# A two-layer graph network on one core: the second attention transposed through DRAM, and three smaller changes

## The chip, the cores and the metric

The kernel runs on one core of a Trainium2 chip. TensorE (PE in the profile; PEld is its weight load) multiplies matrices into PSUM; VectorE (DVE), ScalarE (ACT) and GpSimd (POOL) work element by element; SyncE (SP) issues DMAs. Each engine executes its own list of instructions in order, and waits on semaphores for the others. The metric is the device time of one execution in microseconds. Three runs of the kernel before took 2780.21, 2780.91 and 2783.22 us, median 2780.91.

## The reference

`x` has 64 batches of 256 tokens with 512 features, in float32; `adj` is a 256 x 256 matrix of zeros and ones. Two layers are applied, each with a residual and a layer norm without weights.

```python
# layer 0: eight heads of 64, masked by adj
q, k, v = x @ Wq + bq, x @ Wk + bk, x @ Wv + bv          # per batch 256 x 512
scores = q_h @ k_h.T / 8 + (1 - adj) * -1e9
x = layernorm(x + softmax(scores) @ v @ Wo + bo)
# layer 1: additive graph attention
h = x @ W
e = leaky_relu(s1[:, None] + s2[None, :], 0.2) * adj     # s1 = h @ a1, s2 = h @ a2
x = layernorm(x + elu(softmax(e) @ h + beta * h))
```

## The kernel before

**Tiling.** A batch is two token tiles of 128 partitions (`NT` = 2). Two batches make a pair; q, k and v are computed for a pair (`pair`, L570), everything after them for one batch (`batch`, L634), s = 0 or 1 within the pair. All operands are float32. A product of a weight and the tokens is done in seven block products in place of eight (`project`, L414): sums of weight quarters are kept or streamed from DRAM, and sums of token quarters are made by GpSimd (`token_sums`, L393).

**First layer of a batch.** `scores(c)` (L699) gives transposed scores of two heads; VectorE adds the mask, ScalarE takes the exponential (`pT`), GpSimd adds the two key halves (`both`). `denominators` (L723) sums over keys by TensorE, so that row 16h of the result holds the sums of head h; VectorE takes the reciprocal of the 128 x 256 tile (L735), SyncE stores eight of its rows to DRAM (L746) and loads them back spread over the partitions of their heads (L750). `mix` multiplies by v, `onto` scales by the reciprocals (L776), and the product with Wo is added to `X`, which holds x plus biases.

**Norm.** `norm` (L553) takes one token tile: `bn_stats` and `bn_aggr` on VectorE, two GpSimd operations for the reciprocal root, one of VectorE for the offset, and ScalarE's normalising pass. It is called for each tile after the first layer (L867) and by `finish` (L646) after the second.

**Second layer of a batch.** Since h = xW, s1 and s2 are x times two fixed rows, `wa_sb`; four VectorE products with accumulation give them per token in `sv` (L877). s2 is needed as a row on all partitions: TensorE transposes the broadcast columns (`tr_s`, L887). Then `z` = s1 + s2, leaky ReLU, the mask by GpSimd, maximum, exponential, reciprocal and a scaled sum with beta on the diagonal (L896 to L918) give `e`, the attention of 256 x 256. TensorE transposes it in four blocks (`tr_a`, L923), ScalarE copies it to `attT` (L927), GpSimd makes its quarter sums (L963), and `spread` multiplies it with x, `u` with W. `finish` applies the ELU, adds and norms.

**The first tokens.** x is needed transposed. `blocks` (L583) loads x with the 32 x 32 blocks in transposed places, in runs of 32 elements, four issues for one batch, and one VectorE instruction transposes within the blocks (L591).

**The order.** Nothing is launched as written: each operation is recorded by `plan.op(engine, ns, fn, reads, writes, ...)` with a planned duration, and `Plan.place` (L112) simulates the engines and buffers, and from that fixes the order of every engine's list. TensorE's order is prescribed: `turn(what)` gives each operation a round (the pair's number plus `LATER[what]`) and the place of `what` in `ROUND`; the last 60 TensorE operations are free. The other engines take what can start earliest, ties by a due time derived from TensorE's order. A transfer is planned to land 2200 ns after its issue (`LAG`). Buffers come from pools with fixed numbers of places (`slots`): 18 of the kind `half`, four of `full`, eight PSUM banks. `claims` makes an operation take places for buffers that later ones write.

```python
ROUND = ("sums1", "mix1", "scores0", "v", "o1", "attention0", "u1", "x", "spread0", "sums0", "mix0", "scores1", "q",
         "logits1", "o0", "u0", "attention1", "k", "spread1", "logits0")
```

With `LATER`, a round holds steps of several pairs: sums1, o1, logits1 of the pair before, u1 of the one before that, q and k of the next. So the latency of one batch's steps lies beside TensorE's work for the others. The last batch (`last`) has shorter paths of its own.

## Time and profile before

| what | value |
|---|---|
| runs | 2780.21, 2780.91, 2783.22 us |
| profiled execution | 2782.27 us, span 2780.4 us |
| TensorE clock granted | 0.995 of full speed |
| second layer's transposes on TensorE | 256 `tr_a`, 128 `tr_s` matmuls |
| reciprocal L735 on VectorE | 64, 1757 ns each |
| norm statistics on VectorE | 256 of 681 ns, 256 of 169 ns |
| norm's two GpSimd operations | 256 of 245 ns, 256 of 607 ns |
| VectorE's block transpose of x, L591 | 64, 1232 ns each |
| DMA engines' mean busy share, main queue | 34.0%, 256.96 MB |

How to read it: a span is the time from the first to the last instruction of the profiled execution; the execution's own time is a little longer. A group of instructions stands on one line: line of the kernel, engine, operation, output and inputs by name, shape, count, then the busy time in microseconds and the mean of one in nanoseconds, then the idle time before it with what ended it. A timeline line has the start and the duration in microseconds, then the same names. A line on waits has who waited, for whom, the total in microseconds, how many times, and the longest.

### The profile page before, as it was taken

The page shows a single profiled execution, that of the slowest core. Times are in us where ns is not written, and L with a number is a line of the kernel's source. Part 1 is how long each engine was busy: PE and PEld are TensorE (multiplying, and loading weights), DVE is VectorE, ACT ScalarE, POOL GpSimd, SP SyncE. Part 2 cuts the span into 40 slices and gives each one's busy share as a digit, 9 for nine tenths or more (in the row PEclk, how much of TensorE's full clock was granted, in tenths as well). Part 3 has the DMA queues.
Part 4 walks back from the last instruction along what each step waited for, and adds up shares of the span by engine and source line. Part 5 has one row for each costly group of instructions (what it writes and reads, how often), then busy time and mean ns, then how long its engine had stood idle before and what let it go on. Part 6 is the DMA issues. An engine that isn't in the chain of part 4 may idle for free.

```text
span 2780.4 us, 46736 instructions
## 1 busy us (share of the span) xinstructions
PE 2738.3 (98%) x16259; PEld 2312.2 (83%) x16259; DVE 2067.6 (74%) x4190; ACT 1238.7 (45%) x2747; POOL 1759.1 (63%) x2379
## 2 busy tenths in 40 slices
PE   7999999999999999999999999999999999999997
PEld 6788888888888888888888888888888888888875
DVE  6777777787776777777877767777778777677777
ACT  2344444454454444444544544444445445444443
POOL 5666666666666666666666666666666666666664
PEclk9999999999999999999999999999999999999998
DMA  8333332343332433323433324433234332243211
GB/s 220 88 96 107 81 103 68 101 115 96 84 85 80 115 107 80 103 69 100 114 96 84 84 80 114 107 81 102 68 101 115 95 85 85 81 114 92 62 50 36
DMA packets 429313, 260.02 MB, mean 94 GB/s; under 512 B 279448, under 2 KB 360592, under 8 KB 429072
## 3 DMA queue, kind: packets, MB, share of 16 engines
q1 hardware_dynamic: 428944, 256.96, 34.0%
q8 instruction: 132, 2.16, 0.3%
q14 instruction: 109, 0.89, 0.1%
q0 software_dynamic: 128, 0.01, 0.0%
HBM read 220.73 MB, written 36.17 MB: 92 GB/s over the span
## 4 chain that ended last, share of the span: by engine, by line
PE 97%; DVE 2%; issue 0%; SPq 0%; POOL 0%; DMA 0%; ACT 0%; POOLq 0%; DVEq 0%; ACTq 0%
PE ps_chain L433 33%; PE ps_cross L433 22%; PE ps_pair L433 10%; PE ps_sc L708 8%; PE ps_pv L685 8%; PE ps_second L433 6%; PE ps_fourth L433 6%; PE ps_den L731 2%; PE tr_a L923 1%; PE tr_s L887 0%; DVE junk L877 0%; SPq L588 0%; PE ps_y L938 0%; DVE x L650 0%; PE ps_plain L497 0%
## 5 line engine op out<-in xcount | busy, mean ns | idle before, releaser
L719 POOL TENSOR_TENSOR both<-pT 128x256 f32<-128x256 f32 x512 | 369.2, 749 | 46.2 <-ACT pT L717 46.2
L717 ACT ACTIVATE pT<-pT 128x512 f32<-128x512 f32 x512 | 296.5, 625 | 113.6 <-DVE pT L715 113.4
L715 DVE TENSOR_TENSOR pT<-ps_sc,maskT_sb 128x512 f32<-128x512 f32 x512 | 318.1, 679 | 0.2 <-PE ps_sc L708 0.2
L560 POOL TENSOR_SCALAR rs<-mv 128x1 f32<-128x1 f32 x256 | 62.7, 245 | 351.7 <-DVE mv L557 342.8
L708 PE MATMUL ps_sc<-qT,kT 64*128 64x256 f32 x2048 | 238.4, 382 | 0.0
L685 PE MATMUL ps_pv<-pT,v 128*64 128x256 f32 x2048 | 235.1, 382 | 0.0
L708 PEld LDWEIGHTS ps_sc<-qT,kT 64*128 64x128 f32 x2048 | 192.8, 187 | 44.4 <-issue 24.2
L685 PEld LDWEIGHTS ps_pv<-pT,v 128*64 128x64 f32 x2048 | 141.3, 137 | 91.0 <-issue 25.9
L566 ACT ACTIVATE x<-x,nmr,rs 128x512 f32<-128x512 f32 x256 | 204.0, 811 | 8.1 <-DVE nmr L564 6.5
L877 DVE SCALAR_TENSOR_TENSOR junk<-x,wa_sb 128x512 f32<-128x512 f32 x256 | 195.4, 800 | 0.0
L404 POOL TENSOR_TENSOR yS<-yT 128x256 f32<-128x256 f32 x126 | 103.4, 820 | 144.1 <-DVE yT L478 139.1
L910 ACT ACTIVATE e<-e,nm 128x256 f32<-128x256 f32 x128 | 64.7, 506 | 255.5 <-DVE nm L907 255.5
L561 POOL TENSOR_TENSOR rs<-rs,neg_half 128x1 f32<-128x1 f32 x256 | 155.3, 607 | 21.3
L669 POOL TENSOR_TENSOR x<-x,res_sb 128x512 f32<-128x512 f32 x128 | 161.7, 1284 | 7.8 <-DMA x<-in_x_dram 6.4
L556 DVE BATCH_NORM_STATS2 bn<-x 128x6 f32<-128x512 f32 x256 | 164.2, 681 | 2.2
L963 POOL TENSOR_TENSOR X_sums<-x 128x256 f32<-128x256 f32 x126 | 107.1, 850 | 66.4 <-ACT x L566 66.4
L927 ACT COPY attT<-tr_a 128x512 f32<-128x512 f32 x64 | 37.5, 586 | 244.3 <-PE tr_a L923 243.9
L404 POOL TENSOR_TENSOR xS<-xT 128x512 f32<-128x512 f32 x64 | 81.7, 1277 | 92.6 <-PE ps_chain L433 83.0
L404 POOL TENSOR_TENSOR oS<-oT 128x256 f32<-128x256 f32 x126 | 98.1, 779 | 65.9 <-DVE oT L776 59.7
L905 POOL TENSOR_TENSOR e<-e,adj_sb 128x512 f32<-128x512 f32 (+1 forms) x65 | 82.1, 1263 | 85.5 <-DVE e L902 84.1
L771 ACT COPY oT<-ps_pv 128x512 f32<-128x512 f32 x128 | 75.1, 586 | 131.8 <-PE ps_pv L685 129.6
L433 PE MATMUL ps_chain<-sw_sb,yS 128*128 128x256 f32 x504 | 129.3, 379 | 0.0
(230 smaller groups left out, 7260.1 us busy)
## 6 DMA issues: line engine op xcount, KB each, us to landing
xin<-in_x_dram SPq DMA_DIRECT2D x256, 128.0 KB
x<-in_x_dram SPq DMA_DIRECT2D x64, 512.0 KB
out_dram<-x SPq DMA_DIRECT2D x128, 256.0 KB
inv_all<-rows SPq DMA_DIRECT2D x126, 256.0 KB
wq_sums<-wq_sums SPq DMA_DIRECT2D x124, 256.0 KB
wk_sums<-wk_sums SPq DMA_DIRECT2D x124, 256.0 KB
wq_sums<-in_L_gnn_Wq_dram SPq DMA_DIRECT2D x93, 256.0 KB
wk_sums<-in_L_gnn_Wk_dram SPq DMA_DIRECT2D x93, 256.0 KB
```

Of the source, the lines that this page charges most:

```text
L404: plan.op("POOL", 180 + 545 * width // P, lambda: nc.gpsimd.tensor_tensor(dst(), p(), m(), ALU.subtract), reads, writes)
L433: nc.tensor.matmul(dst[:, f, :], lhs, rhs, start=start and f == 0 and c == 0, stop=c == inner - 1, skip_group_check=True)
L556: plan.op("DVE", 690, lambda: nc.vector.bn_stats(bn[A], X[:, t, :]), [(X, (t, 0)), (X, (t, 1))], [bn])
L561: nc.gpsimd.tensor_tensor(rs[A], rs[A], neg_half, ALU.pow)
L566: plan.op("ACT", 810, lambda: nc.scalar.activation(X[:, t, :], X[:, t, :], AF.Identity, bias=nm[A], scale=rs[A]), [nm, rs], [(X, (t, 0)), ...
L669: plan.op("POOL", 1270, lambda t=t: nc.gpsimd.tensor_tensor(X[:, t, :], X[:, t, :], res_sb[A], ALU.add), [res_sb], tokens(t))
L685: nc.tensor.matmul(acc[r * HD:(r + 1) * HD, i, :], V[:, 2 * k + s, h * HD:(h + 1) * HD], pT[h][:, k, :], start=k == 0, stop=k == NT - 1)
L708: nc.tensor.matmul(acc[j][:, k, :], kT[r:r + HD, c, key_blk(k)], own(qT, r, c), start=True, stop=True)
L715: plan.op("DVE", 690, lambda h=h, i=i: nc.vector.tensor_add(pT[h][A], acc[i][A], maskT_sb[A]), [acc[i], maskT_sb], [pT[h]])
L717: plan.op("ACT", 620, lambda h=h: nc.scalar.activation(pT[h][A], pT[h][A], AF.Exp, scale=1.0 / HD ** 0.5), [pT[h]], [pT[h]])
L719: plan.op("POOL", 725, lambda h=h, i=i: nc.gpsimd.tensor_tensor(both[c][:, i, :], pT[h][:, 0, :], pT[h][:, 1, :], ALU.add), [pT[h]], [(bot ...
L877: plan.op("DVE", 780, lambda t=t, i=i, junk=junk: nc.vector.scalar_tensor_tensor(junk[A], X[:, t, :], 1.0, wa_sb[:, i, :], op0=ALU.mult, o ...
```

## The change

Five things are altered.

1. For all but the last batch the attention `e` is stored to DRAM (`square`) and loaded in four strided issues with its 32 x 32 blocks in transposed places (`att_b`); one VectorE instruction transposes within the blocks into `attT`. TensorE's four transposes and ScalarE's copy go. The step keeps a place in TensorE's order, with no instruction in it.
2. The row of logits s2 is stored to DRAM from `sv` (`line`, 256 single elements) and loaded as a row on all partitions (`row`), in place of two TensorE transposes.
3. `norm` takes both token tiles at once: sums by ScalarE's accumulator, then squares of the difference from the mean likewise, one small scaling by VectorE, three GpSimd operations on 128 x 2, and ScalarE's normalising passes. `finish` does both tiles before it norms; the last batch still goes tile by tile.
4. The denominators are copied by ScalarE as they are, stored to DRAM, loaded as 128 x 16 (`few`), inverted there, stored again and then spread.
5. The first pair's x is loaded plainly and transposed by TensorE (`turned`). `ROUND` has another order, new pools `few`, `line` and `square` are declared, and some planned durations differ.

```diff
-ROUND = ("sums1", "mix1", "scores0", "v", "o1", "attention0", "u1", "x", "spread0", "sums0", "mix0", "scores1", "q",
-         "logits1", "o0", "u0", "attention1", "k", "spread1", "logits0")
+ROUND = ("sums1", "mix1", "scores0", "u1", "attention0", "v", "spread0", "o1", "sums0", "mix0", "scores1", "u0", "x",
+         "logits1", "attention1", "q", "o0", "logits0", "k", "spread1")
...
-    def norm(X, t):
-        bn, mv, rs, nm = st(6, "bn"), st(2, "mv"), st(1, "rs"), st(1, "nmr")
-        plan.op("DVE", 690, lambda: nc.vector.bn_stats(bn[A], X[:, t, :]), [(X, (t, 0)), (X, (t, 1))], [bn])
-        plan.op("DVE", 175, lambda: nc.vector.bn_aggr(mv[A], bn[A]), [bn], [mv])
+    def norm(X, ts):
+        n = len(ts)
+        sums, mean, sq, rs, nm = (st(n, name) for name in ("sum", "mean", "sq", "rs", "nmr"))
+        def total(i, t, func, to, bias):
+            junk = sb("half", [D], "junk")
+            plan.op("ACT", 700, lambda: nc.scalar.activation(
+                junk[A], X[:, t, :], func, bias=mean[:, i:i + 1] if bias else 0.0, accum_out=to[:, i:i + 1]),
+                [(X, (t, 0)), (X, (t, 1))] + ([mean] if bias else []), [junk, (to, i)])
+        for i, t in enumerate(ts):
+            total(i, t, AF.Identity, sums, False)
+        plan.op("DVE", 110, lambda: nc.vector.tensor_scalar(mean[A], sums[A], -1.0 / D, None, ALU.mult), [sums], [mean])
+        for i, t in enumerate(ts):
+            total(i, t, AF.Square, sq, True)
         def rsqrt():
-            nc.gpsimd.tensor_scalar(rs[A], mv[:, 1:2], EPS, None, ALU.add)
-            nc.gpsimd.tensor_tensor(rs[A], rs[A], neg_half, ALU.pow)
-        plan.op("POOL", 800, rsqrt, [mv], [rs])
-        plan.op("DVE", 150, lambda: nc.vector.scalar_tensor_tensor(
-            nm[A], mv[:, 0:1], -1.0, rs[A], op0=ALU.mult, op1=ALU.mult), [mv, rs], [nm], mode="two")
-        plan.op("ACT", 810, lambda: nc.scalar.activation(
-            X[:, t, :], X[:, t, :], AF.Identity, bias=nm[A], scale=rs[A]),
-            [nm, rs], [(X, (t, 0)), (X, (t, 1))])
+            nc.gpsimd.tensor_scalar(rs[A], sq[A], 1.0 / D, EPS, ALU.mult, ALU.add)
+            nc.gpsimd.tensor_tensor(rs[A], rs[A], neg_half[A].to_broadcast([P, n]), ALU.pow)
+            nc.gpsimd.tensor_tensor(nm[A], mean[A], rs[A], ALU.mult)
+        plan.op("POOL", 1000, rsqrt, [sq, mean], [rs, nm])
+        for i, t in enumerate(ts):
+            plan.op("ACT", 810, lambda i=i, t=t: nc.scalar.activation(
+                X[:, t, :], X[:, t, :], AF.Identity, bias=nm[:, i:i + 1], scale=rs[:, i:i + 1]),
+                [nm, rs], [(X, (t, 0)), (X, (t, 1))])
...
+        def turned(s):
+            rows = sb("xin", [NT, D], f"xin_{m}_{s}")
+            for t in range(NT):
+                plan.op("SP", 700, lambda t=t: nc.sync.dma_start(rows[:, t, :], dram(x, s)[:, t, :]), [], [(rows, t)],
+                        first=s == 0 and t == 0)
+                tr = ps([C, P], "tr_x")
+                def pe(t=t, tr=tr):
+                    for c in range(C):
+                        nc.tensor.transpose(tr[:, c, :], rows[:, t, blk(c)], ident)
+                plan.op("PE", 430, pe, [(rows, t)], [tr], claims=[xT])
+                plan.op("ACT", 680, lambda t=t, tr=tr: nc.scalar.copy(xT[:, :, blk(2 * t + s)], tr[A]), [tr],
+                        [(xT, (t, s))])
...
         turn("x")
-        plan.op("PE", 0, lambda: None, [], [(xT, "turn")], claims=[xT])
-        for s in range(2):
-            blocks(s)
+        if m == 0:
+            for s in range(2):
+                turned(s)
+        else:
+            plan.op("PE", 0, lambda: None, [], [(xT, "turn")], claims=[xT])
+            for s in range(2):
+                blocks(s)
...
-        def finish(t, us, u, mode):
...
-            norm(X, t)
-            plan.op("SP", 1400, lambda: nc.sync.dma_start(
-                dram(out, s)[:, t, :], X[:, t, :]), tokens(t), [])
+        def finish(ts, us, u, mode):
+            for t in ts:
...
+            norm(X, ts)
+            for t in ts:
+                plan.op("SP", 700, lambda t=t: nc.sync.dma_start(dram(out, s)[:, t, :], X[:, t, :]), tokens(t), [])
...
-            rows = Buf(dram_pool, "rows", [H, N], "rows")
+            rows = Buf(dram_pool, "rows", [2, H, N], "rows")
...
-                plan.op("DVE", 1750, lambda: nc.vector.reciprocal(inv[A], acc[A]), [acc], [inv])
...
+                def sum_of(i, src, n, to):
+                    plan.op("ACT", 240 + n, lambda: nc.scalar.activation(
+                        to[:, 0:n], src[:, 0:n], AF.Identity, accum_out=range_sb[:, i, b:b + 1]), [src],
+                        [to, (range_sb, (i, b))])
-                plan.op("SP", 60, lambda: nc.sync.dma_start(rows[A], inv[0:P:P // H, :]), [inv], [rows])
+                n = H * N // P
+                few, one = sb("few", [n], "few"), sb("few", [n], "one")
+                sum_of(0, acc, N, inv)
+                plan.op("SP", 500, lambda: nc.sync.dma_start(rows[0], inv[0:P:P // H, :]), [inv], [(rows, 0)])
+                plan.op("SP", 500, lambda: nc.sync.dma_start(
+                    few[A], rows[0].rearrange("h (a n) -> (h a) n", n=n)), [(rows, 0)], [few])
+                plan.op("DVE", 190, lambda: nc.vector.reciprocal(few[A], few[A]), [few], [few])
+                sum_of(1, few, n, one)
+                plan.op("SP", 500, lambda: nc.sync.dma_start(
+                    rows[1].rearrange("h (a n) -> (h a) n", n=n), few[A]), [few], [(rows, 1)])
...
-                    plan.op("SP", 1500, spread, [rows], [(everywhere, i)])
+                    plan.op("SP", 1000, spread, [(rows, 1)], [(everywhere, i)])
...
-        for t in range(NT):
-            norm(X, t)
+        for ts in ([0], [1]) if last else ([0, 1],):
+            norm(X, ts)
...
-        sv = [st(2, "s") for t in range(NT)]
+        sv = st(2 * NT, "s")
...
-                    accum_out=sv[t][:, i:i + 1]), tokens(t) + [(wa_sb, i)], [junk, (sv[t], i)],
+                    accum_out=sv[:, NT * i + t:NT * i + t + 1]), tokens(t) + [(wa_sb, i)], [junk, (sv, (i, t))],
...
-        row = ps([N], "tr_s")
-        def pe_row():
-            for t in range(NT):
-                nc.tensor.transpose(row[:, blk(t)], sv[t][:, 1:2].to_broadcast([P, P]), ident)
...
+        attT = sb("half", [NT, N], "attT")
+        s2 = [(sv, (1, t)) for t in range(NT)]
         turn("logits")
-        plan.op("PE", 220, pe_row, sv, [row], claims=[z, e])
+        if last:
+            row = ps([N], "tr_s")
+            def pe_row():
+                for t in range(NT):
+                    nc.tensor.transpose(row[:, blk(t)], sv[:, NT + t:NT + t + 1].to_broadcast([P, P]), ident)
+            plan.op("PE", 220, pe_row, s2, [row], claims=[z, e])
+        else:
+            line, row = Buf(dram_pool, "line", [N], "line"), sb("half", [N], "row")
+            plan.op("PE", 0, lambda: None, [], [(row, "turn")], claims=[z, e, row])
+            with_turn = [(row, "turn")]
+            plan.op("SP", 500, lambda: nc.sync.dma_start(
+                line[A].rearrange("(t p) -> p t", p=P), sv[:, NT:2 * NT]), s2 + with_turn, [line])
+            plan.op("SP", 500, lambda: nc.sync.dma_start(row[A], row_on_all(line[A], 0, N)), [line], [row])
...
-                z[:, t, :], row[A], sv[t][:, 0:1], None, ALU.add), [row, sv[t]], [(z, t)])
+                z[:, t, :], row[A], sv[:, t:t + 1], None, ALU.add), [row, (sv, (0, t))], [(z, t)])
...
-            def pe_att(ts=ts):
-                for j in range(NT):
-                    for t in range(NT)[ts]:
+        turn("attention")
+        if last:
...
+        else:
+            square, att_b = Buf(dram_pool, "square", [N, N], "square"), sb("half", [NT, N], "att_b")
+            plan.op("PE", 0, lambda: None, [], [(att_b, "turn")], claims=[attT, att_b])
+            plan.op("SP", 500, lambda: nc.sync.dma_start(
+                square[A].rearrange("(t p) j -> p t j", p=P), e[A]), [e], [square])
+            for f in range(4):
+                plan.op("SP", 720, lambda f=f: nc.sync.dma_start(
+                    att_b[f * 32:(f + 1) * 32].rearrange("p k (b i) -> p k b i", i=32),
+                    square[A].rearrange("(b j) (k f i) -> f j k b i", j=32, f=4, i=32)[f]),
+                    [square, (att_b, "turn")], [(att_b, f)])
+            plan.op("DVE", 660, lambda: nc.vector.transpose(attT[A], att_b[A]), [att_b], [(attT, i) for i in range(4)])
...
-        for t in range(NT):
-            finish(t, [(u, (t, 0)), (u, (t, 1))], lambda t=t: u[:, t, :], "two")
+        finish(range(NT), lambda t: [(u, (t, 0)), (u, (t, 1))], lambda t: u[:, t, :], "two")
```

## The prediction

> **What bounds the kernel now.** I read the page's head and chain first, then who TensorE waited for, then its timeline in the steady middle, then the DMA queue there, and last the two ends.
>
> ```profile
> span 2780.4 us, 46736 instructions
> PE 2738.3 (98%) x16259; PEld 2312.2 (83%) x16259; DVE 2067.6 (74%) x4190; ACT 1238.7 (45%) x2747; POOL 1759.1 (63%) x2379
> ...
> PE 97%; DVE 2%; issue 0%; SPq 0%; POOL 0%; DMA 0%; ACT 0%; POOLq 0%; DVEq 0%; ACTq 0%
> ```
>
> A busy share alone proves little, but the chain that ended last is 97% TensorE as well. The waits of TensorE give the rest: each occurs once, so none belongs to the loop.
>
> ```profile
> PE ps_chain L433 <- DVE xT L591: 12.5, 1, 12.5
> PE ps_chain L433 <- DVE pT L715: 6.4, 1, 6.4
> PE ps_pair L433 <- DVE nmr L564: 4.0, 1, 4.0
> PE tr_a L923 <- POOL rs L560: 3.6, 1, 3.6
> ```
>
> The first is the start, the second the filling of the pipeline (65 to 71.5 us), the last two lie after 2700 us. In between, TensorE's instruction list sets the time. The chain in order of time shows the same head's scores 84.95 us apart in successive pairs of batches; 31 to 32 such rounds make the span.
>
> ```profile
> 1246.94 3.65 PE ps_sc L708 x32
> 1295.68 3.65 PE ps_sc L708 x32
> 1331.89 3.65 PE ps_sc L708 x32
> ```
>
> TensorE's timeline shows what the second layer's transposes take: the distance from their start to the next group's start (printed durations overlap, since matmuls are pipelined).
>
> ```profile
> 1231.68 1.03 PE L433 MATMUL ps_chain<-so_sb,oS 128*128 128x256 f32 x4
> 1232.54 0.60 PE L923 MATMUL tr_a<-ident,e 128*128 128x128 f32 x4
> 1232.98 1.03 PE L433 MATMUL ps_chain<-w_sb,yT 128*128 128x256 f32 x4
> ...
> 1262.71 0.38 PE L887 MATMUL tr_s<-ident,s 128*128 128x128 f32 x2
> 1262.93 1.03 PE L433 MATMUL ps_chain<-wo_sb,oT 128*128 128x256 f32 x4
> ```
>
> So four transposes of the attention take 0.44 us and the two of the row of logits 0.22 us.
>
> The DMA queue, for the price of a hop through DRAM:
>
> ```profile
> 1242.24 2.80 SPq L588 DMA_DIRECT2D xin<-in_x_dram  x4
> 1245.70 0.62 SPq L746 DMA_DIRECT2D rows<-inv  x1
> 1247.59 1.30 SPq L750 DMA_DIRECT2D inv_all<-rows  x2
> ```
>
> A store to DRAM followed by a load of it costs 1247.59 - 1245.70 = 1.9 us for the store. Four strided issues of `xin` take 2.80 us, 0.70 each.
>
> **The change, part by part.** (1) Transposes off TensorE: 63 of the 64 batches (the last keeps its path) lose 0.44 + 0.22 = 0.66 us, 63 x 0.66 = 41.6 us, all on the bounding engine. The sequence of the tile modes (sums, mix, scores adjacent, twice a round) is the same, so no switch is added.
>
> (2) What covers the new way. Group times from the timeline: sums 1.0, mix 3.6, scores 3.65, o, u 6.05 each, q, k, v 12.1 to 12.2 each, spread 3.1. In the new ROUND the second layer of batch s=1 has, from the end of o1 to spread1, sums0, mix0, scores1, u0, q, o0, k: 44.6 us. Batch s=0 has, from o0 to spread0, k, spread1, sums1, mix1, scores0, u1, v: 41.7 us. What must fit in it:
> - Norm: last addition 0.42; two sums on ScalarE, by the Exp of the same shape (629 ns) and an accumulator read (188 ns) 0.82 each; scaling 0.15; two squares 0.95 each (between that 0.82 and L566's 811 ns plus 188); GpSimd 245 + 607 ns and one more small operation, 1.1 for both tiles; two normalisings 1.62; hand-overs 0.8. Sum 7.6.
> - The four products of L877, 0.88 each with their reads: 3.5.
> - Row of logits: store and broadcast load, two hops of 1.9 to 2.5: 4.4. The store has 256 runs of 4 bytes, which no row has; from below one small hop (1.9), from above a strided `xin` issue and landing. At the start eight of those, issued from 0.74, had landed by 11.16 with the last issue ending at 8.17, so 0.93 + 3.0 = 3.9. I take 2.2.
> - Softmax: 0.95 + 0.73 + 1.27 + 0.68 + 1.39 + 0.15 + 1.19 and 0.7 of hand-overs: 7.1.
> - Attention: store 1.9, four strided loads at 0.70 to 0.93 each, landing 1.9 to 3.0, VectorE's block transpose 0.62 (half of L591's 1232 ns): 7.3, between 6.0 and 9.2.
>
> Together 30 us with the engines free. They aren't: in this trace the softmax ran from 1263.5 to 1272.3 (8.8) and, beside the scores, from 1291.2 to 1304.9 (13.6), so 2 to 7 more: 32 to 37. That leaves 5 to 12 us. I cost parts 1's replacement at nothing; the cover is those groups, and if it were gone each microsecond over it would cost TensorE one.
>
> (3) Engines. VectorE loses per batch a reciprocal (1757 to about 150 ns), four statistics (681 + 169 ns), four `nmr` (223 ns), and gains 0.62 and two scalings: 5.1 us less, 63 times 320, to about 1750 us. ScalarE gains eight passes (7.0), loses the `attT` copy (0.59) and most of a range sum (0.4): 6.0 us more, to about 1620 us (59%). GpSimd loses about 1 us a batch. None bounds. Queued behind ScalarE's new passes are the exponentials of the scores and the copies out of PSUM; 6 us in 42 is within its idle 55%.
>
> (4) Reciprocals: sums to o now hold four hops (store, load, store, broadcast) and VectorE's 0.15 in place of 1757 ns and two hops. 0.6 + 2.2 + 2.2 + 0.3 + 2.0 + 3.3, two multiplications of 0.9, four GpSimd sums of 0.78: 15.5 us, against 25.4 us from sums0 to o0 and 28.5 from sums1 to o1. Hidden; without that cover, 4 us a batch.
>
> (5) SyncE's queue: per batch nine new issues (row 2, attention 5, reciprocals 2), about 0.6 each, 5.4 us, and out stores moved behind a joint norm. The issues of a round here sum to some 21 us; 32 of 84 leaves room. Behind a waiting issue stand `wq_sums` and `wk_sums`, which q and k await, and `xin`; four dependent hops a batch at 1.27 us of wait add 10 us a round. Small pieces on the DMA engines: in 1242 to 1250 they were busy 0.50 x 16 x 8 = 64 us for at least the 4096 pieces of four `xin`, so at most 16 ns each; 2048 a batch make 2 us of all 16 engines. The share goes from 0.34 to about 0.45.
>
> The row is that block loads as `xin` (128-byte runs) hide in every round. The Trainium skill speaks against: "DMA: Bandwidth & Descriptors", Rules for kernel authors, puts a transposition by rearranged access at 19 times the hardware transpose, and one descriptor to an element where the last dimension is strided. Were the attention's loads 19 times 256 KB at the 200 GB/s seen here (1.3 us), they would take 24 us, overrun by 10 and make the kernel some 600 us slower. Only the 4-byte store has that form here, so I follow the row.
>
> (6) Start. The first x comes in four plain 256 KB loads, transposed by TensorE (four groups of 0.44, at half clock 0.88: the first matmuls here take 3.78 us where 1.89 is usual) and copied by ScalarE. Before, the two DVE transposes waited until 11.16 and TensorE began at 12.46. `wq_sb`'s four issues took 2.09, so x and `wq` are issued by 0.74 + 4.2 = 4.9 instead of 10.3; the loads move 2 MB, at 200 GB/s 10 us. I take 4 us gained; between 6 gained (the issue time saved) and 2 lost (the transposes, with the copies).
>
> (7) Filling. The first batch has no u1 and spread1 for cover, 32.5 us against 32 to 37: 2 us lost, between 0 and 5. Drain: the last batch's two norms get 1 us longer each (ScalarE in series), and batch 62 has the long chain with less behind it, but about 19 us are lost there already to idle and slow clock. I take 2 lost, between 8 gained and 10 lost.
>
> Sum: -41.6 - 4 + 2 + 2 = -41.6 us. The profiled execution took 2782.27 us (1.9 around its span), 1.4 above the median of 2780.91; 2740.7 there, 2739 at the median.
>
> **Rivals.**
> - *Partly covered, 0.14.* SyncE or a burst (the DMA share was 0.77 from 1258 to 1266) delays some batches by 0.2 to 0.5 us on average, or the ends cost their bounds: 20 us less gain, 2760. For it: 5 us is thin. Against: no engine is over 0.65.
> - *Equal, 0.04.* The same with 0.66 a batch.
> - *The DRAM chain becomes the bound, slower, 0.17.* Place: spread0, which comes 41.7 us after o0. It decides when the chain passes 41.7 + 1.3 = 43 us (1.3 a round is all that is saved). With every one of its four hops at twice 1.9, 37 + 7.6 = 44.6: 2.9 us a round, 31 rounds, 90 us, 2829. For it: hops queue behind weight and x loads in the same queue, and no landing times are shown. Against: `xin` and `inv_all` almost never kept VectorE waiting (2.2 and 1.0 us in all).
> - *Square needs another activation table, 0.05.* The trace has one ACT_TABLE_LOAD (1.28 us) and no Square. Two a norm, 127 norms, 325 us: ScalarE at 1950 us still isn't the bound, but the chain grows by 2.6, to 40: 2739 to 2800. By the skill's "ScalarE: Activation LUTs", What ACT_TABLE_LOAD costs, a switch is 2.66 us, so 5.3 a norm and the chain at 42.
>
> **How the numbers follow.** Forecast 0.60, with its own range from the ends' bounds (14 gained, 17 lost): 2725 to 2756. The range reaches into the slower cases until under 0.2 is outside: 2724 to 2795. No change that can be told is within 0.2% (5.6 us). Faster 0.60 + 0.14 + 0.01 of the table case, slower the rest.
>
> **What would show it.** Right: no `tr_a`, `tr_s` of 0.66 us a batch; the scores' spacing 83.6 instead of 84.95; TensorE's chain still 97%; no repeated wait at `ps_chain<-attT`; ScalarE near 59%, VectorE near 63%; one table load. Wrong: TensorE waiting 60 times on VectorE's `attT` transpose, on `oT`, or on weights; matmuls at half speed after waits; SyncE waiting long at the new stores; a first matmul later than 12.5.

## The result and the profile after

The changed kernel takes 3134.15 us, median of four runs (3099.1 to 3140.81), against 2781.33 us beside it: 1.124 times as long, 95% interval 1.116 to 1.133. The forecast was 2739, the range 2724 to 2795. The profiled execution took 3140.81 us.

The head of the page after, its chain by engine, and the start of the chain by line:

```profile
span 3139.0 us, 47485 instructions
PE 2855.4 (91%) x15897; PEld 2342.8 (75%) x15897; DVE 1825.0 (58%) x3613; ACT 1554.6 (50%) x3712; POOL 1720.8 (55%) x2257
...
PE 46%; DMA 27%; DVE 10%; POOL 7%; ACT 5%; issue 3%; SPq 1%; POOLq 0%; DVEq 0%
PE ps_chain L433 18%; DMA line<-s 15%; PE ps_cross L433 13%; DMA row<-line 8%; PE ps_pair L433 7%; PE ps_second L433 4%; ACT junk L560 3%; POOL both L750 3%; DMA wq_sums<-wq_sums 2%; PE ps_fourth L433 2%; DVE junk L922 2%; DVE pT L746 2%; POOL X_sums L1030 1%; PE ps_pv L716 1%; DVE qT L478 1%
```

TensorE has 362 matmuls fewer and yet is busy 117 us longer: its granted clock fell from 0.995 to 0.953. By these shares the slow clock took 0.047 of 3139 us, less 0.005 of 2780 before: an estimated 130 us at most, since part of it fell into waits. The chain that was 97% TensorE is now 46%. The two hops of the row of logits, `line<-s` and `row<-line`, hold 23% of it. The waits after (who, for whom, total us, times, longest) say the same from three engines:

```profile
DVE z L950 <- DMA row<-line: 402.9, 62, 9.6
SPq L947 <- DMA line<-s: 376.7, 63, 8.3
PE ps_chain L433 <- DVE x L899: 74.9, 30, 3.7
PE ps_chain L433 <- DVE pT L746: 65.3, 30, 4.7
PE ps_cross L433 <- DVE pT L746: 27.6, 29, 1.5
PE ps_chain L433 <- DMA wq_sums<-wq_sums: 20.4, 22, 1.7
```

VectorE stood still 6.5 us 62 times, once a batch, at the row's first use; SyncE waited 6 us each time to issue the second hop; and TensorE, which waited for nothing in the loop before, now waits for VectorE some 30 times in each of several places. One such place in the chain in order of time (start, duration, what):

```profile
1488.70 8.61 DMA line<-s
1497.31 0.02 issue
1497.32 5.69 DMA row<-line
1503.01 0.02 issue
1503.04 0.04 DVE z L950
...
1503.31 1.28 DVE qT L478 x2
1504.59 0.60 DVE x L683
1505.19 0.62 DVE junk L922 x2
...
1506.83 0.42 DVE x L899
1507.25 0.14 issue
1507.39 2.04 PE ps_chain L433 x4
```

The store of 256 elements, one kilobyte in all, takes 8.6 us, and the load behind it 5.7. VectorE's timeline around that:

```profile
1495.35 1.03 DVE L683 SCALAR_TENSOR_TENSOR x<-m,x 128x512 f32<-128x512 f32 x1
1503.04 0.35 DVE L950 TENSOR_SCALAR z<-row,s 128x256 f32<-128x256 f32 x1 [6.67 <-DMA row<-line]
```

VectorE is free from 1496.4 and waits for `z`. The two `qT` stand in its list behind `z`, though TensorE has made their operands by 1494.2 and 1497.6. They are done only when the row is there, and so the addition of the product with Wo (`x L899`), whose operand is ready at 1503.1, comes only at 1506.83. These additions free the PSUM banks that TensorE needs. TensorE's timeline shows what that does:

```profile
1502.02 1.03 PE L433 MATMUL ps_chain<-wo_sb,oT 128*128 128x256 f32 x4
...
1503.75 1.03 PE L433 MATMUL ps_pair<-wo_sb,oT 128*128 128x256 f32 x4
1507.39 2.04 PE L433 MATMUL ps_chain<-so_sb,oS 128*128 128x256 f32 x4 [2.62 <-DVE x L899]
1509.32 1.85 PE L433 MATMUL ps_cross<-so_sb,oT 128*128 128x256 f32 x4
1511.01 1.03 PE L433 MATMUL ps_pair<-wo_sb,oS 128*128 128x256 f32 x4
```

A wait of 2.62 us, then two groups at half speed (2.04 and 1.85 us for 1.03): the granted clock was 1.00 until 1507.3 us and 0.55 from there to 1511.1. The Trainium skill's "TensorE: Matmul & The Clock Gate", The HAM clock gate, has the clock halved after about 3.4 us of idling; here 2.62 us in one wait were followed by it, so the measurement is what I go by.

By the starts of the groups, the round from the o behind q at 1407.0 us to the next such o at 1502.0 took 95.0 us; before, 84.95; forecast, 83.6. The excess over the forecast, 11.4 us, is in five steps: o 12.1 instead of 6.05, u 8.8 for 6.05, q 13.2 for 12.1, spread 4.2 for 3.15, scores 4.3 for 3.65. In this round the waits in spread, scores and u are for VectorE, and that in q is for a piece of weights (`wq_sums`). In o, 2.8 us of the 6 lost are the wait and 3.3 the slow groups behind it. 31 times 11.4 is 353 us; most of the rest of the 395 us between forecast and result is in rounds that lost more, such as that from the scores at 1574.6 to those at 1672.0, 97.4 us. The median distance from scores to the same scores a pair later is 96.6 us.

### The profile page after: what moved, and what is told of

The parts are those of the page before. It is cut to its first block, busy times and chain, and to the rows that moved or that the text cites. A ratio compares the mean times of both kernels' runs of the same rounds, so it can differ in the third digit from the quotient of the medians.

```text
span 3139.0 us, 47485 instructions
## 1 busy us (share of the span) xinstructions
PE 2855.4 (91%) x15897; PEld 2342.8 (75%) x15897; DVE 1825.0 (58%) x3613; ACT 1554.6 (50%) x3712; POOL 1720.8 (55%) x2257
## 4 chain that ended last, share of the span: by engine, by line
PE 46%; DMA 27%; DVE 10%; POOL 7%; ACT 5%; issue 3%; SPq 1%; POOLq 0%; DVEq 0%
PE ps_chain L433 18%; DMA line<-s 15%; PE ps_cross L433 13%; DMA row<-line 8%; PE ps_pair L433 7%; PE ps_second L433 4%; ACT junk L560 3%; POOL both L750 3%; DMA wq_sums<-wq_sums 2%; PE ps_fourth L433 2%; DVE junk L922 2%; DVE pT L746 2%; POOL X_sums L1030 1%; PE ps_pv L716 1%; DVE qT L478 1%
## 5 line engine op out<-in xcount | busy, mean ns | idle before, releaser
L750 POOL TENSOR_TENSOR both<-pT 128x256 f32<-128x256 f32 x512 | 409.2, 831 | 42.0 <-ACT pT L748 41.8
L560 ACT ACTIVATE junk<-x 128x512 f32<-128x512 f32 x256 | 160.5, 627 | 488.7 <-DVE x L683 274.6
L950 DVE TENSOR_SCALAR z<-row,s 128x256 f32<-128x256 f32 x126 | 42.5, 360 | 404.0 <-DMA row<-line 402.9
L404 POOL TENSOR_TENSOR oS<-oT 128x256 f32<-128x256 f32 x126 | 125.0, 992 | 250.3 <-DVE oT L821 245.4
L922 DVE SCALAR_TENSOR_TENSOR junk<-x,wa_sb 128x512 f32<-128x512 f32 x256 | 228.8, 927 | 6.1 <-ACT x L577 6.1
L560 ACT ACTIVATE junk<-x,mean 128x512 f32<-128x512 f32 x256 | 183.7, 718 | 79.9 <-DVE mean L566 79.9
L433 PE MATMUL ps_chain<-so_sb,oS 128*128 128x256 f32 x504 | 147.8, 420 | 74.9 <-DVE x L899 74.9
L433 PEld LDWEIGHTS ps_chain<-so_sb,oS 128*128 128x128 f32 x504 | 103.9, 211 | 102.5 <-issue 82.0
L566 DVE TENSOR_SCALAR mean<-sum 128x2 f32<-128x2 f32 (+1 forms) x130 | 51.5, 396 | 173.0 <-ACT junk L560 171.0
L433 PE MATMUL ps_chain<-w_sb,yT 128*128 128x256 f32 x252 | 80.4, 447 | 67.4 <-DVE pT L746 60.6
```

The source lines that it names most:

```text
L404: plan.op("POOL", 180 + 545 * width // P, lambda: nc.gpsimd.tensor_tensor(dst(), p(), m(), ALU.subtract), reads, writes)
L433: nc.tensor.matmul(dst[:, f, :], lhs, rhs, start=start and f == 0 and c == 0, stop=c == inner - 1, skip_group_check=True)
L560: plan.op("ACT", 700, lambda: nc.scalar.activation(junk[A], X[:, t, :], func, bias=mean[:, i:i + 1] if bias else 0.0, accum_out=to[:, i:i ...
L750: plan.op("POOL", 725, lambda h=h, i=i: nc.gpsimd.tensor_tensor(both[c][:, i, :], pT[h][:, 0, :], pT[h][:, 1, :], ALU.add), [pT[h]], [(bot ...
L922: plan.op("DVE", 780, lambda t=t, i=i, junk=junk: nc.vector.scalar_tensor_tensor(junk[A], X[:, t, :], 1.0, wa_sb[:, i, :], op0=ALU.mult, o ...
```

## The experiments

Names used below: "runs of 32" is the changed kernel with one store altered (e4), "the base" is e4 with the norm of before (e6), the fastest kernel of the study. Times are medians; ratios are to the kernel before in the same session, with their 95% interval.

**1. Is it the row of logits, and does the order of steps matter?** Three kernels: the row made by TensorE again with the old `ROUND` (e1), the kernel before with nothing but the row through DRAM (e2), and the changed kernel whose order was planned with the store landing 6 us later (e3).

```diff
 e1: -        if last:                       # row by TensorE, and ROUND of before
     +        if not general:
 e2: (on the kernel before)
     -        plan.op("PE", 220, pe_row, sv, [row], claims=[z, e])
     +            plan.op("SP", 500, ... line.rearrange("(t p) -> p t"), sv[:, NT:2 * NT] ..., [line])
     +            plan.op("SP", 500, ... row, row_on_all(line, 0, N) ..., [line], [row])
 e3: +            plan.extra[len(plan.ops) - 1] = 6000.0     # planned landing of line<-s
```

> The changed kernel with the row of logits by TensorE's two transposes again and the order of before (the new order leaves no room for that step); attention through DRAM, norm by ScalarE, small reciprocals and the plain first load stay. If the store of single elements costs the time: TensorE saves only 63 x 0.44 = 27.7 us, so 2754, within 2735 to 2780. If the attention through DRAM or ScalarE's norm costs it: above 2950. If the new order alone costs it: also about 2754, which e4 tells apart.

> The kernel before with nothing changed but the row of logits through DRAM. If the store of single elements (8 to 9 us until the load may start) costs the time: the row comes some 13 us after the products, against 12 us of o0 and u0 between logits1 and attention1, and VectorE waits for it with its reads of PSUM behind: slower than before, 2900 to 3300. If it is not the store: 2781 - 63 x 0.22 = 2767, 2755 to 2785.

> The changed kernel, the same operations, but the planner is told that the store of the row takes 6 us longer to land, so that it may place other work of VectorE ahead of z. If the harm is the order of VectorE's list (z too early, PSUM reads behind it): most of the 400 us come back, 2740 to 2820. If the harm is the latency itself or the DMA engines' time that the store holds: 2850 to 3100. If it is anything else: 3100 to 3140.

Measured: e1 2806.66 us (1.0088, 1.0068 to 1.0108); e2 3219.55 (1.157, 1.155 to 1.160); e3 3276.18 (1.178, 1.175 to 1.180). The row through DRAM alone makes the old kernel 16% slower, with the same wait as in the changed kernel. Waits of e2, then of e3:

```profile
DVE z L906 <- DMA row<-line: 426.4, 63, 9.3
SPq L901 <- DMA line<-s: 376.1, 63, 9.0
PE ps_pair L433 <- DVE u L478: 173.3, 30, 8.1
PE ps_cross L433 <- DVE pT L715: 123.1, 29, 6.4
```

```profile
DVE z L952 <- DMA row<-line: 294.3, 61, 11.7
PE ps_chain L434 <- DVE x L900: 179.0, 28, 7.3
PE ps_chain L434 <- DMA wq_sums<-wq_sums: 46.1, 24, 3.4
```

Planning for a later landing only moved the wait: VectorE stood 109 us less at `z`, and TensorE lost more elsewhere. So a wrong planned duration isn't the whole cause. e1, without the store, was still slower than before, and 53 us short of what I expected: something else in the change costs too.

**2. The form of the store.** The same 1 KB, but VectorE first spreads s2 over 32 columns and transposes within 32 x 32 blocks, so that eight runs of 32 elements are stored in place of 256 single elements.

```diff
+            plan.op("DVE", 130, ... wide, sv[:, NT:2 * NT].unsqueeze(2).to_broadcast([P, NT, 32]) ...)
+            plan.op("DVE", 150, lambda: nc.vector.transpose(turned_s[A], wide[A]), [wide], [turned_s])
-                line[A].rearrange("(t p) -> p t", p=P), sv[:, NT:2 * NT]), s2 + with_turn, [line])
+                line[A].rearrange("(t b i) -> b t i", t=NT, i=32), turned_s[0:P:32]), [turned_s] + with_turn, [line])
```

> The changed kernel with the store of the row in 8 runs of 32 elements instead of 256 single ones: VectorE spreads s2 over 32 columns and transposes within 32 x 32 blocks (two instructions, some 0.3 us), and four partitions are stored. If the single elements cost the time: the hop falls from 8 to 9 us to about 2, and the forecast's 2739 comes, 2725 to 2765. If the order, the attention through DRAM or ScalarE's norm costs it: above 3050.

Measured: 2787.72 us, 1.002 (1.001 to 1.003). Of the loss, 346 us came back by this one store. The issue of the second hop now follows that of the first by 2.9 us in the median over 63 batches (8.8 in the changed kernel, both from the queue's timeline), and the second lands in 3.2 us for 4.9 (medians of the 17 and 14 landings that the traces hold). What is left over my forecast is 49 us; its profiled execution, at 2782.55, was the fastest of ten. A pair there takes 85.07 us in the median: the 1.32 us of transposes are gone, and as much has come back, 0.8 us of it (25.0 us over 31 rounds) in these small repeated waits of TensorE:

```profile
PE ps_chain L433 <- POOL xS L404: 12.0, 27, 0.9
PE ps_pair L433 <- DVE yT L478: 6.8, 17, 0.7
PE ps_cross L433 <- POOL attT L1034: 6.2, 10, 1.1
```

**3. Why single elements are slow.** First half as many: t = 0 as 128 single elements, t = 1 in runs of 32.

```diff
+                line[A].rearrange("(t p) -> p t", p=P)[:, 0:1], sv[:, NT:NT + 1]), s2 + with_turn, [(line, 0)])
+                line[A].rearrange("(t b i) -> b t i", t=NT, i=32)[:, 1:2], turned_s[0:P:32, 1:2]), ... [(line, 1)])
```

> The kernel with the row in runs of 32 elements, but for half of it: the row of t = 0 leaves SBUF as 128 single elements of 4 bytes, that of t = 1 in 4 runs of 32. Theory S, the store's time goes with the number of single elements (256 took 8 to 9.6 us, that is about 0.5 us for each of the 16 that an engine has): 128 take 4 to 5 us from issue to landing, z waits about half of the 9.6 us that it waited with 256, and the time is in between, 2850 to 2980 us. Rival, a fixed cost of the form (a strided store is slow however many elements it has): as with all 256, 3100 to 3200 us. Rival, a threshold (the half store fits into the cover that the prediction counted): 2785 to 2800 us. Its own landing time decides between the first two.

Measured: 3133.64 us in one run, as with all 256, and again 8.8 us from the store's issue to that of the next hop. Theory S, that the time goes with the number, fell. In the trace's packet records of the changed kernel, the 4-byte packets of the store issued at 1488.70 run from 1490.5 to 1491.5 us at about 10 ns each, and the next hop starts at 1497.32. The time lies behind the packets, not in them. The Trainium skill's "DMA: Bandwidth & Descriptors", Two DMAs through the same engine are not ordered, says that a DMA engine's reading and writing sides are separate queues. These numbers would agree with a write that is late behind its read; no run here shows which side is late.

Then three kernels that differ in one number. To the base is added a second store of the same 256 elements, which the row's load waits for, with the elements 512 bytes, 64 bytes or 4 bytes apart in DRAM:

```diff
+            far = Buf(dram_pool, "far", [N * w], "far")        # w = 128, 16 or 1
+            plan.op("SP", 500, lambda: nc.sync.dma_start(
+                far[A].rearrange("(t p w) -> p t w", p=P, w=w)[:, :, 0:1], sv[:, NT:2 * NT].unsqueeze(2)), ..., [far])
-            plan.op("SP", 500, ... row, row_on_all(line[A], 0, N) ..., [line], [row])
+            plan.op("SP", 500, ... row, row_on_all(line[A], 0, N) ..., [line, far], [row])
```

> The fastest kernel so far (row in runs of 32 elements, norm of before on VectorE: 2742.3 us) plus one store more per batch: the same 256 elements of 4 bytes, each to a place of its own 512 bytes from the next, which the load of the row waits for. In the slow stores the packets of 4 bytes are all sent within about 1 us, at 9 to 11 ns each, yet the store is done only 6 us later, and 128 of them last as long as 256 with 128 to each 512 bytes. Theory P, elements that share a place of DRAM are written one after the other: spread out, the store is done within 2 to 3 us of its issue, like the one of 128 pieces of 64 bytes, and the time is 2742 to 2775 us. Rival F, a write of 4 bytes is slow wherever it goes: the store lands 8 us after its issue again and the time is 3000 us or more.

> The fastest kernel (2742.3 us) plus the store of 256 single elements that the row's load waits for, the elements 64 bytes apart in DRAM (512 bytes apart it was 2743.6 us). If elements have to share 64 bytes to hold each other up: 2740 to 2750 us. If sharing 512 bytes is enough (8 elements each): more than side by side has per element, in between, 2760 to 2950 us.

> The same addition with the 256 elements side by side, 1024 bytes in all, as the changed kernel has them. Theory P (elements that share a place are written one after the other): the row's load starts 8 to 9 us after the store and the time is near that of the changed kernel without its ScalarE norm, about 3090 us (2980 to 3150). Rival, the slow store needs something else of the changed kernel (its norm, its order of VectorE): 2743 to 2760 us.

Measured, one run each: 2743.6 us at 512 bytes, 2741.02 at 64, 3137.77 side by side; the base without the store is 2742.3. SyncE's queue, first with 64 bytes between the elements, then side by side:

```profile
1420.49 0.36 SPq L945 DMA_DIRECT2D far<-s  x1
1423.56 0.57 SPq L942 DMA_DIRECT2D line<-turned_s  x1
1425.58 0.32 SPq L948 DMA_DIRECT2D row<-line  x1
```

```profile
1432.06 0.41 SPq L945 DMA_DIRECT2D far<-s  x1
1434.40 0.57 SPq L942 DMA_DIRECT2D line<-turned_s  x1
1443.49 0.32 SPq L947 DMA_DIRECT2D row<-line  x1
```

5.1 us against 11.4 from the store `far` to the load; over all 63 batches the medians are 4.6 and 11.5. With 64 bytes between the elements the load follows the store of `line` by 2.6 us in the median, as in e6 without `far`. Number of elements, size, engine, order and dependence are the same; only the distance differs. That is shown: 256 elements of 4 bytes cost nothing measurable when each has 64 bytes for itself, and 395 us of the kernel when they lie side by side. That writes into the same 64 bytes are done one after the other (16 in each, 8.8 / 16 = 0.55 us apiece, which would also explain why half as many took as long) is argued from these, not shown; a distance between 4 and 64 bytes wasn't run.

The Trainium skill's "DMA: Bandwidth & Descriptors", Specifications, puts full rate at 512 bytes and has smaller transfers read, modify and write. No time follows from it here: elements of 4 bytes at 64 bytes' distance paid nothing.

**4. What takes back the saving: norm and attention.** Runs of 32 with the norm of before, `bn_stats` on VectorE (e6); and with the second attention turned by TensorE (e7).

```diff
 e6: -        for i, t in enumerate(ts): total(i, t, AF.Identity, sums, False) ... total(i, t, AF.Square, sq, True) ...
     +        for t in ts: norm_one(X, t)             # norm of before
 e7: -        if last:                                # attention
     +        if not general:
```

> The kernel with the row of logits stored in runs of 32 elements (2787.7 us, a pair of elements 84.9 us) plus the norm statistics of before (bn_stats and bn_aggr on VectorE in place of the two accumulating passes on ScalarE). Theory N, the norm on ScalarE takes back the saving: its two added passes per row block (627 and 718 ns with their accumulator reads) stand in front of ScalarE's reads of PSUM (the yT and v copies, the exponentials), and the small waits of u and spread (about 1.5 us of a pair) come from there; they go, and the pair falls to 83.6 us: 2787.7 - 31 x 1.3 = about 2747 us (2740 to 2760). Rival, VectorE's room: 690 + 175 + 150 ns per block come back to VectorE, 6 blocks of a pair, some 6 us of a pair on an engine that is already 67% busy and whose PSUM additions are already what spread waits for: 2790 to 2830 us. If neither counts: 2783 to 2792 us.

> The kernel with the row in runs of 32 elements, with the second attention turned by TensorE and VectorE's copy as before (tr_a, 63 batches of 0.44 us on TensorE = 27.7 us more work there), the rest unchanged. Theory A, the way of attT through DRAM is what the small waits come from (its POOL products, its transfers among the weights): the waits of u and spread go and pay for tr_a: 2780 to 2795 us, no slower than without. Rival, the saving of tr_a is real and the waits have another cause: 2787.7 + 27.7 = about 2815 us (2808 to 2825). In between: the share of tr_a that was worth something.

Measured: e6 2742.3 us, 0.9861 (0.9846 to 0.9876): 1.4% faster than the kernel before, and faster than runs of 32. The time is theory N's, and the small waits of e4 are gone; VectorE's room was no matter. That ScalarE's reads of PSUM were what stood behind the added passes isn't shown by this run, since work on GpSimd and the tying of two row blocks went with them. Head and chain of e6, then its chain in order of time, where the same head's scores are 83.76 us apart:

```profile
span 2739.1 us, 47358 instructions
PE 2701.9 (99%) x15897; PEld 2269.9 (83%) x15897; DVE 2084.5 (76%) x4377; ACT 1202.6 (44%) x2688; POOL 1767.5 (65%) x2379
...
PE 96%; DMA 1%; DVE 1%; POOL 1%; issue 0%; ACT 0%; SPq 0%; POOLq 0%; DVEq 0%
```

```profile
1302.25 3.65 PE ps_sc L732 x32
...
1386.01 3.65 PE ps_sc L732 x32
```

VectorE is busier than before (76% for 74%), and TensorE waits for it nowhere in the loop.

e7 took 3300.34 us, 1.186 (1.185 to 1.188): neither theory. Its waits tell why:

```profile
PE tr_a L984 <- DVE e L974: 472.5, 33, 16.0
PEld tr_a L984 <- POOL nmr L573: 465.5, 29, 16.4
```

The new `ROUND` has the step `attention0` right behind u1. As an empty place for a transfer that costs nothing; with TensorE's transposes in it, TensorE stands 14 us there until the softmax is done. The run measured the order of steps, not the attention. So the question was put again, on the base with the old `ROUND` (e13), beside the norm alone on the kernel before (e12), and, later, runs of 32 with the new norm one row block at a time (e15):

```diff
 e13: e7's edit on the base, and ROUND of the kernel before
 e12: (on the kernel before) norm(X, ts) by ScalarE; norm(X, [t]) in finish, norm(X, [0, 1]) after attention
 e15: -            norm(X, ts)
      +            for t in ts: norm(X, [t])           # and likewise after attention
```

> The fastest kernel so far (2742.3 us) with the second attention turned by TensorE again, in the order of steps of the kernel before. In the earlier run with TensorE's transposition the new order put it right behind scores and u, and TensorE waited there some 14 us for the normalised weights 33 times: that run measured the order. Here 63 batches of 0.44 us come back to TensorE and nothing waits: 2742.3 + 27.7 = 2770 us (2766 to 2778). Rival: the attention's way through DRAM was worth more or less than its 0.44 us, because the PSUM copies by VectorE and ScalarE come back too (2780 to 2800 us) or because its DMA had cost waits (2745 to 2760 us).

> The kernel before (2782 us) with one edit: the norm statistics by ScalarE, both row blocks together after attention, one at a time at the end of the layer. Theory N, the norm on ScalarE costs by itself what it cost beside the other edits (2787.7 against 2742.3 us, 1.46 us of a pair): 2815 to 2835 us. Rival, it costs only in the new order of steps, where u and scores follow other work: 2778 to 2790 us. My prediction counted it as hidden: 2782 us.

> The kernel with the row in runs of 32 elements and the norm on ScalarE (2787.7 us), but the norm of each row block by itself: the sums, the mean and the factors of block 0 no longer wait for block 1. Theory G, the tying of two blocks is what costs in the new order: 2742 to 2760 us. Theory N, ScalarE's and GpSimd's added work is what costs (GpSimd gets three small operations per block instead of per two, some 1.1 us per two blocks more): 2785 to 2815 us.

Measured: e13 2780.64 us (0.9995, 0.9985 to 1.0004); e12 2799.1 (1.0061, 1.0044 to 1.0078); e15 2776.92 (0.9981, 0.9971 to 0.9991).
- Attention through DRAM, with the order that goes with it, is worth 2780.6 - 2742.3 = 38 us, 10 more than the 27.7 of its transposes. A pair of e13 takes 84.90 us for 83.7: 0.87 of transposes, and 0.5 in the spread behind one of them (3.62 us for 3.14). Part of the 38 lies ahead of the loop, whose first scores come at 105.1 us for 98.4 in e6. The time falls on the lower edge of the rival's range (more than 0.44 us a batch); that the copies out of PSUM are the reason, as the rival had it, isn't shown.
- The norm on ScalarE costs 17 us by itself and 45 us in the new order. e12 was outside both expectations, between them: a pair goes from 84.95 to 85.71 us, in spread (3.52), scores (3.81) and o (6.36), as waits.
- e15 fell between its theories as well: without the tying of two row blocks 11 of the 45 us are gone, and 34 stay with ScalarE's and GpSimd's added work. Its scores still take 4.29 us in every second place, 3.65 elsewhere.

**5. The start and the reciprocals.** The kernel before with only the new first loads (e10), and the base with the reciprocals of before, 128 by 256 (e14).

```diff
 e10: +        if m == 0: turned(s) ... else: blocks(s) ...
 e14: -                few = ... rows[0] -> few, reciprocal(few), few -> rows[1]
      +                plan.op("DVE", 1750, lambda: nc.vector.reciprocal(inv[A], acc[A]), [acc], [inv])
      +                for i, d in enumerate((acc, inv)): sum_of(i, d, N, sb("half", [N], "junk"))
      +                plan.op("SP", 500, ... rows[1], inv[0:P:P // H, :] ..., [inv], [(rows, 1)])
```

> The kernel before with one edit: the first pair's x is loaded plainly and turned by TensorE, all else as before. The new kernel's start began its scores 11 us earlier (98.70 us against 109.89 us). Theory: that gain stands by itself, since the fill is on the chain that sets the end and the pairs behind it only shift: 2782.3 - 11 = about 2771 us (2768 to 2776). Rival: the pairs behind it meet the weights, which still come at their own rate, and the gain is taken back as waits for them in the first pairs: 2780 to 2784 us. My prediction counted 4 us for this start: 2778 us.

> The fastest kernel so far (2742.3 us) with the reciprocals of the kernel before, 128 by 256 on VectorE, one store instead of three hops. My prediction had both ways hidden under the same cover: 2739 to 2746 us. Rival, VectorE's room: at 76% busy, 1.6 us more per batch (4 to 5 points) delays its reads of PSUM, as ScalarE's norm did: 2760 to 2790 us.

Measured: e10 2778.07 us, 0.9988 (0.9979 to 0.9997): 3.9 us gained, as the prediction had it and not the 11 expected of the scores' start. e14 3120.31 us, 1.122 (1.119 to 1.125), far beyond either expectation. The waits of TensorE in e14, and VectorE's timeline at one of them:

```profile
PE ps_chain L433 <- POOL oT L404: 100.1, 30, 3.4
PE ps_pair L433 <- DVE u L478: 71.5, 30, 2.7
PE ps_chain L433 <- ACT u L469: 61.1, 30, 2.1
```

```profile
1387.18 4.87 DVE L739 TENSOR_TENSOR pT<-ps_sc,maskT_sb 128x512 f32<-128x512 f32 x8
1391.97 1.78 DVE L808 TENSOR_TENSOR oT<-oT,inv_all 128x512 f32<-128x512 f32 x2
1393.67 0.68 DVE L909 SCALAR_TENSOR_TENSOR junk<-x,wa_sb 128x512 f32<-128x512 f32 x1
...
1398.48 0.41 DVE L478 TENSOR_TENSOR u<-ps_pair,u 128x256 f32<-128x256 f32 x1
```

One store in place of a store, a load and a store brings the reciprocals early, and the planner, which takes what can start earliest, puts `oT` and the four products of L909 ahead of the additions of u. TensorE has made u's first products by 1392.3 and waits; u takes 11 to 13 us instead of 6.1. None of TensorE's repeated waits there is for a transfer; by this trace the list's order is the cost. No run isolates it from VectorE's added time, and e14 doesn't say that 1.5 us more of VectorE are worth 378 us in another order.

## Why the prediction was wrong

**Step 2, the row of logits: here it failed.** I priced its two hops at 4.4 us, with 1.9 and 3.9 as bounds of the store, taken from a store of eight whole rows and from strided loads. Measured: 8.8 us to the next issue, 4.9 for the load, 13.7 together. I wrote that no row has 256 runs of 4 bytes, and still let rows that store long runs, or that write to SBUF, set the upper end. No bound can come from a row that lacks the property in question. The number of runs, which I did see, wasn't that property: at 64 bytes' distance the same 256 were free.

**Step 2, what lies on the path.** I let each microsecond over the cover cost TensorE one, at the end of the chain, spread. 9.3 us more on a chain of 32 to 37 us would overrun the covers of 41.7 and 44.6 us by at most 5 us. In the round above spread lost 1 us; o, u and scores lost 9.4, since the chain's wait stood in VectorE's list ahead of additions that free PSUM banks, and q lost 1.1 to a late piece of weights. Nor did a microsecond cost one: in o a wait of 2.8 us cost 6, with the groups at half speed behind it. I asked what was queued behind ScalarE's new passes, and not what was queued behind `z`, whose operand now came from a transfer. In e4, where VectorE still waits 3 us a time at `z` (110.1 us in 36 waits), TensorE has no repeated wait left for `x`, `pT` or `qT`: 3 us are covered and 6.5 are not.

**The rival that a DRAM chain becomes the bound** was the right kind and had 0.17; its mechanism, four hops each at twice the price, and its place, spread0, were not. One hop at four times the price, and a blocked VectorE, made 3134, not 2829. The rival of the activation table is out: the profile after has one table load, as before.

**Step 1, right.** With the store mended and the old norm, a pair takes 83.75 us in the median (83.6 forecast), and TensorE's chain is 96% of the span.

**Step 3, wrong by 45 us.** "None bounds" held, and ScalarE at 50% had room. The norm cost 17 us on the old kernel and 45 here, where I had put it at nothing. My reading is that its added passes stand ahead of copies and exponentials that others await in turn, and that GpSimd's and VectorE's work starts later; only the tying of two row blocks was run apart.

**Step 5** held for the attention: the 128-byte pieces take 13 ns each in the packet records (at most 16 forecast), and its four loads land in 2.9 us each (median of the 30 landings that the trace holds, of 252 loads; 3.2 in e6). It didn't hold for the queue behind the slow store: `wq_sums` landed in 8.4 us, and TensorE waited 20.4 us for it in 22 waits.

The rule that I weighed there, the Trainium skill's "DMA: Bandwidth & Descriptors", Rules for kernel authors, would by its factor of 19 have made an estimated 25 us of these loads (I wrote 24). No run here shows such a cost for runs of 128 bytes.

**Step 4** was right for the new way: in e6 TensorE doesn't wait for it in the loop. It gave the old way no price; in the new order that way costs 378 us.

**Steps 6 and 7.** The start was 4 us by itself, as taken. In e6 the first scores of the loop come 11.5 us earlier (98.39 for 109.89), and the wait of 6.4 us in the filling is gone, where I had put a loss of 2; the drain is 6.9 us longer (96.0 for 89.1), for 2 taken. With 36.7 gained in the loop they make 41.3 us, beside a forecast of 41.6: the sum fits e6 in part by luck, since its terms at the ends are off and make up for a loop that gained less than 41.6.

## What to carry to other kernels

Price a store by where its pieces land, not by its bytes: single elements put side by side in DRAM are a form of their own, and until it has been measured its upper bound is open. Where a column must become a row in DRAM, let VectorE transpose 32 x 32 blocks first and store runs of 128 bytes, or give each element 64 bytes. And when an operand begins to come from a transfer, read the in-order list behind its first reader: what that engine would have freed meanwhile is the price, however far off the critical path the chain itself lies.

## What the runs showed of the hardware

- 256 elements of 4 bytes to DRAM side by side: 8.8 us from issue to the next hop's issue; 128 of them likewise; 256 at a distance of 64 or 512 bytes, no measurable cost; eight runs of 128 bytes, 2.9 us.
- A transfer's packets can be recorded as finished some 6 us before its completion reaches the engine that waits: the last of the store's 4-byte packets about 1491.5 us, the next hop at 1497.32.
- TensorE's granted clock can halve after a wait of 2.62 us: 1.00 before 1507.3 us, 0.55 in the 3.8 us behind it.
- Other transfers land later in the changed kernel than in e4, which differs from it in the form of that store: the row's load in 4.9 us instead of 3.2, the pieces of `wq_sums` in 8.4 instead of 2.7.
